# Layer 1's convolution in a four-layer graph network on one core: the product with adj² in two places a quarter, last sums by DMA and VectorE, 0/1 blocks as bytes

## The chip, the cores and the metric

The kernel runs as one program on one core of a Trainium2 chip. The metric is device time in microseconds (us); lower is better. The core has five engines that run their own instruction streams in order: TensorE (PE in the profile, with its weight loads as PEld), VectorE (DVE), ScalarE (ACT), GpSimd (POOL) and SyncE (SP), which issues most DMA transfers. An instruction that waits holds up everything behind it on its engine. SBUF is the on-chip memory of 128 partitions; matmul results land in PSUM, which has 8 banks of 128 partitions x 512 fp32 numbers.

## The reference

Four residual layers over x of shape (8, 2048, 64): 8 batches, 2048 nodes, 64 features. Each normalises x, applies a ReLU and adds a graph layer. adj is a 0/1 matrix of 2048 x 2048, sparse except near its first rows and columns. The change is in layer 1 and in how adj is kept for layers 1 and 2:

```python
def _L1_gnn_ref(x, A, embedding, weight, bias):
    K = weight.shape[1]                                  # 3
    w = jnp.einsum('nd,dkio->nkio', embedding, weight)   # d: 16
    b = jnp.einsum('nd,do->no', embedding, bias)
    As = [jnp.eye(N, dtype=x.dtype), A]
    As.append(2.0 * (A @ As[-1]) - As[-2])
    A_stack = jnp.stack(As, 0)
    x_g = jnp.einsum('knm,bmc->bnkc', A_stack, x)
    out = jnp.einsum('bnki,nkio->bno', x_g, w)
    return out + b

h = jnp.maximum(_layernorm(x, axis=-1), 0.0)
x = x + _L1_gnn_ref(h, adj, L1_gnn_embedding, L1_gnn_weight, L1_gnn_bias)
```

So each node has its own weights, a mix of 16 matrices by its embedding. Layer 2 multiplies adj with a message three times (`adj @ v`), with two small dense maps around it.

## The kernel before

**Layout.** Features lie on partitions in pairs of batches: 4 quarters q, each 128 partitions (2 batches x 64 features) by 2048 nodes. Nodes come in 16 target tiles of 128 and in 4 chunks of 512 (4 tiles). An array "by nodes" has 128 nodes on partitions and 512 columns (8 batches x 64).

**The sparse product** (class `Feed`). For one target tile t the product adj x is summed in one PSUM bank `acc`: first three dense source tiles (`dense`, the "hubs": 3 tiles, each in a high and a low part, so 6 matmuls), then `LISTED[t]` listed groups of 128 gathered source rows (7 to 3 for t from 1 to 15), each 2 matmuls; tile 0 takes 13 whole source tiles instead. A listed group is fetched into `raw` (POOL's indirect DMA, line 2578; for tile 0 SP's plain DMA, line 2576), split into `part_hi` (ACT, line 2595) and `part_lo` (DVE, line 2596), and multiplied with 0/1 weights. The weights are cast by ACT from adj blocks kept in bf16: `cells` and `zero` (line 2554) and `dense` (line 2564). `ahead` is how many groups are split before the one in use, `raws` how many fetch buffers there are, `group` how many blocks one cast takes. `finish` adds the node's own row (`own`, an SP load) and leaves `z`.

**The convolution** (`convolution_near`). `product(place)` computes adj (adj h) for one chunk, turned to features by four transposes a tile (`turn`) into `aah`. Chunk order is 1, 0, 2, 3 ("places" 0 to 3). While place p is convolved, `product(p + 1)` runs in between, cut into pieces by its `yield`s; `product(0)` runs alone, ahead of the loop.

In a place there are 4 quarters, and in each 4 block groups (`blk` 0, 2, 4, 6; two blocks of 2 embedding entries each). A block group is 4 PSUM banks `pk` (of 6): 4 matmuls with `w01` (128 rows) and, after a piece of the product, 4 with `w2` (64 rows each, on `aah`); an fp32 matmul shows as two passes. VectorE then does 4 times `y = (pk + bias) * emb` (line 1834), and GpSimd sums y into two accumulators `half` (line 1840; the first block needs no sum, the last block's two sums are VectorE's). There are 3 buffers for y. A block's 128 partitions are two embedding entries of 64 outputs, so a quarter ends with a sum over the two 64-partition halves of each accumulator: `fold_up` does it on TensorE with a 128 x 64 matrix `fold`, into the two halves of one PSUM bank, and VectorE adds that bank to x (line 1736).

**What sets the order.** `advance()` runs the pieces of the next product: 30 of a place's 32 hooks (two in each block group, one between the w01 and the w2 matmuls, one after) each take their even share of `pieces(place + 1)`, mostly one or none. `waiting` is a list of small functions run one at each block group's end (in the last place, two a group, with the 12 messages for layer 2 among them). It holds `fold_up` two group ends after its quarter's end, then `first` (store x, start the normalisation) and the rest of it. On top of this the framework's scheduler orders each engine's stream. The SP queue carries `own`, `raw` of tile 0, the embedding loads of the next place (line 1776, `q<-in_embT_dram` in the profile), and x in and out.

Of the kernel before, what the change touches and what calls it, by code (L numbers as in the profile page):

```python
# [7 lines left out]
F = mybir.dt.float32  # L8
BF = mybir.dt.bfloat16
# [10 lines left out]
P = 128  # L20
NB = 8
N = 2048
D = 64
NP = NB // 2
NT = N // P
R = P // NP
CW = 512
NC = N // CW
TC = CW // P
# [13 lines left out]
HUBS = 3  # L43
FAR = NT - HUBS
LISTED = [0, 7, 6, 5, 4, 4, 4, 4, 4, 4, 3, 3, 3, 3, 3, 3]
PLACE = [sum(LISTED[:t]) for t in range(NT + 1)]
F16 = mybir.dt.float16


COLS = ["a_node", "a_gn", "a_ge", "fcb", "av", "b1", "b2", "iv", "bias3"]  # L50
# [84 lines left out]
class Kernel:  # L135
# [1543 lines left out]
    def convolution_near(self, slots, k):  # L1679
        nc, tc, a = self.nc, self.tc, self.a  # L1680
        xe, xo = self.chebyshev(slots)
        lists, steps, ident = self.lists, self.steps, self.ident
        lo, hi = slice(0, D), slice(D, P)
# [3 lines left out]
        for i, order in enumerate(((0, 1), (1, 0))):  # L1687
            t = k.tile([P, DO], F, name=f"w01_{i}")
# [15 lines left out]
                a["bias1"].rearrange("(b j) o -> j o b", j=2)[j],  # L1704
            )

        fold = k.tile([P, D], F, name="fold")
        nc.vector.tensor_add(fold, ident[:, lo], ident[:, hi])

        with (  # L1710
            tc.tile_pool(reuse_waits="tile", name="conv", bufs=2) as w,
            tc.tile_pool(reuse_waits="tile", name="conv_ps", bufs=1, space=PSUM) as ps,
# [4 lines left out]
            chunks = [1, 0, 2, 3]  # L1717
            emb = slots.tile([P, NBLK, CW], F, name="emb", tag="q4")
            two = slots.tile([P, 2, NP, CW], F, name="two", tag="q5")
            aahs, x = (two[:, 0], w.tile([P, NP, CW], F, name="aah", bufs=1)), two[:, 1]  # L1720
            waiting = []
# [7 lines left out]
            def side():  # L1729
                return ps.tile([P, CW], F, name="side")  # L1730

            def fold_up(q, accs):
                po = side()
                for i, h in enumerate((lo, hi)):
                    self.mm(po[h], fold, accs[i])
                nc.vector.tensor_add(x[:, q], po, x[:, q])

            def message(t):
                pn = steps.first_message(v, t, bank())
                self.send(0, t, pn, lists.hub, w)  # L1740

            feed = Feed(
                self, lists, w, self.sent[1], None, raws=4, casts=2, ahead=1, group=2,
                targets=[ch * TC + i for ch in chunks for i in range(TC)],
            )

            def product(place):
                ch, aah = chunks[place], aahs[place % 2]

                def turn(i, z):  # L1750
                    pz = side().rearrange("p (q n) -> p q n", q=NP)
                    for q in range(NP):
                        nc.tensor.transpose(pz[:, q], z[:, q * P : (q + 1) * P], ident)
                    nc.scalar.copy(aah[:, :, i * P : (i + 1) * P], pz)

                last = None
                for i in range(TC):
                    t = ch * TC + i
                    own = feed.own(t)
                    acc = ps.tile([P, CW], F, name="acc")  # L1760
                    feed.dense(acc, t, lists.hub)
                    yield
                    for n, _ in enumerate(feed.listed(acc, t)):
                        if n == 1 and last is not None:
                            turn(*last)
                        yield
                    z = w.tile([P, CW], F, name="z")
                    feed.finish(z, own, acc, t)
                    last = i, z
                    yield  # L1770
                turn(*last)
# [10 lines left out]
                        ),  # L1782
                    )

            def pieces(place):
                targets = [chunks[place] * TC + i for i in range(TC)]
                return sum(2 + (LISTED[t] or FAR) for t in targets)

            for blk in range(0, NBLK, 2):
                load_emb(0, blk)  # L1790
            nc.sync.dma_start(x, self.xs[1][chunks[0]])
# [3 lines left out]
            for place, ch in enumerate(chunks):  # L1795
                s = slice(ch * CW, (ch + 1) * CW)
                aah = aahs[place % 2]
                ends = place == NC - 1
                ahead = iter(()) if ends else product(place + 1)
                many, hook = 0 if ends else pieces(place + 1), 0  # L1800

                def advance():
                    nonlocal hook
                    for _ in range(many * hook // 30, many * (hook + 1) // 30):
                        next(ahead, None)
                    hook += 1

                if ends:
                    for c in chunks[:-1]:
                        for t in range(c * TC, (c + 1) * TC):  # L1810
                            waiting.append(lambda t=t: message(t))
                for q in range(NP):
                    accs = [w.tile([P, CW], F, name="half", bufs=4) for _ in range(2)]
                    sides = list(enumerate(((xe, hi), (xo, lo))))
                    for blk in range(0, NBLK, 2):
                        pks = {}
                        for b in (blk, blk + 1):
                            for half, (src, h) in sides:
                                pk = bank()
                                pks[b, half] = pk  # L1820
                                c = slice(b * P, (b + 1) * P)
                                self.mm(pk, w01[half][:, c], src(q)[:, s], stop=False)
                        advance()
                        if ends and waiting:
                            waiting.pop(0)()
                        for b in (blk, blk + 1):
                            for half, (src, h) in sides:
                                c = slice(b * P, (b + 1) * P)
                                self.mm(pks[b, half], w2[h, c], aah[h, q], start=False)
                        for b in (blk, blk + 1):  # L1830
                            for half in range(2):
                                acc = accs[half]
                                y = acc if b == 0 else w.tile([P, CW], F, name="y", bufs=3)
                                nc.vector.scalar_tensor_tensor(  # L1834
                                    y, pks[b, half], bias[:, b : b + 1], emb[:, b],
                                    op0=OP.add, op1=OP.mult,
                                )
                                if b > 0:
                                    add = nc.vector if b == NBLK - 1 else nc.gpsimd
                                    add.tensor_add(acc, acc, y)  # L1840
                        if q == NP - 1 and not ends:
                            load_emb(place + 1, blk)
                        advance()
                        if waiting:
                            waiting.pop(0)()
                    waiting[:0] = [lambda: None, lambda q=q, accs=accs: fold_up(q, accs)]
                for _ in ahead:
                    pass
                std = w.tile([P, CW], F, name="std", tag="y", bufs=3)
                norm = self.norm_parts(ch, x, Part(v, s), Part(u, s), std, bank, write)  # L1850

                def first(place=place, ch=ch, norm=norm):
                    self.store_x(1, ch, x)
                    next(norm)
                    if place + 1 < NC:
                        nc.sync.dma_start(x, self.xs[1][chunks[place + 1]])

                waiting[2:2] = [first, lambda: None, lambda norm=norm: next(norm, None)]
# [513 lines left out]
class Lists:  # L2372
# [99 lines left out]
    def fill(self, pool, w):  # L2472

        nc = self.nc
        rows = self.kern.a["adjT"].rearrange("j (t n) -> (j t) n", n=P)
        self.cells = pool.tile([P, PLACE[NT], P], BF, name="cells")
        group, late = 4, []

        def keep(s, n, raw):
            self.kern.behind(nc.vector.tensor_tensor(  # L2480
                self.cells[:, s], raw, self.there[:, s].unsqueeze(2).to_broadcast([P, n, P]),
                op=OP.mult,
            ))

        for c in range(0, PLACE[NT], group):
            n = min(group, PLACE[NT] - c)
            raw = w.tile([P, group, P], F, name="listed_raw", bufs=4)[:, :n]
            for i in range(n):
                self.kern.behind(nc.gpsimd.indirect_dma_start(  # L2489
                    raw[:, i], None, rows,  # L2490
                    bass.IndirectOffsetOnAxis(ap=self.cell[:, c + i : c + i + 1], axis=0),
                ))
            late.append((slice(c, c + n), n, raw))
            if len(late) > 2:
                keep(*late.pop(0))
            yield
        for x in late:
            keep(*x)
        yield

    def open(self, pool):
        self.dense = pool.tile([P, HUBS, N], BF, name="dense")
        self.zero = pool.tile([P, FAR, P], BF, name="zero")
        self.hub = Hub(pool, "hub")

    def load(self, w):
# [623 lines left out]
```

## Time and profile before

| | |
|---|---|
| median of 6 runs | 1979.81 us |
| lowest, highest | 1972.23, 1984.59 us |
| the profiled execution | 1974.29 us |
| its span, first to last instruction | 1972.5 us |
| mean granted TensorE clock | 0.911 |
| layer 1's convolution with `product(0)`, about | 735 to 1268 us of the span |
| `raw<-sent,index` gathers | 300, 1050 ns of POOL each |
| loads `dense_raw` of 1024 KB | 3, 5.9 us to landing each |

"Span" is the time between the first and the last instruction of the profiled execution. A row of a group of instructions reads: line of the kernel, engine, operation, output<-inputs, partitions x elements and types, count, then busy time and mean ns of one, then how long the engine stood idle just before these instructions and what ended the idle time. In a stage table each pair is busy us and, in brackets, the number of instructions. In a timeline a row is start, duration, engine, line and what it does; several alike in a row are merged.

### The profile page before, as it was taken

The page shows a single profiled execution, that of the slowest core. Times are in us where ns is not written, and L with a number is a line of the kernel's source. Part 1 is how long each engine was busy: PE and PEld are TensorE (multiplying, and loading weights), DVE is VectorE, ACT ScalarE, POOL GpSimd, SP SyncE. Part 2 cuts the span into 40 slices and gives each one's busy share as a digit, 9 for nine tenths or more (in the row PEclk, how much of TensorE's full clock was granted, in tenths as well). Part 3 has the DMA queues.
Part 4 walks back from the last instruction along what each step waited for, and adds up shares of the span by engine and source line. Part 5 has one row for each costly group of instructions (what it writes and reads, how often), then busy time and mean ns, then how long its engine had stood idle before and what let it go on. Part 6 is the DMA issues. An engine that isn't in the chain of part 4 may idle for free. (4 is left out here: it accounts for less than half of the span.)

```text
span 1972.5 us, 22337 instructions
## 1 busy us (share of the span) xinstructions
PE 1698.7 (86%) x7066; PEld 970.0 (49%) x7066; DVE 1409.5 (71%) x2389; ACT 809.6 (41%) x1627; POOL 1030.3 (52%) x959
## 2 busy tenths in 40 slices
PE   6859889998997787999999999769889998679875
PEld 2425666665324554444443444447667565345432
DVE  6778778884677674877677557589889676458864
ACT  5712344454664653221121010256566754267300
POOL 1100166776870753875765545266474641478760
PEclk8868899998996898999999989789989999689887
DMA  9740223345335876233141210378788774666655
GB/s 345 263 120 1 77 75 103 111 125 180 99 101 173 246 228 177 81 91 107 49 117 33 70 48 38 110 217 253 244 260 268 231 257 168 225 177 176 182 173 190
DMA packets 124057, 305.20 MB, mean 155 GB/s; under 512 B 29312, under 2 KB 31120, under 8 KB 118160
## 3 DMA queue, kind: packets, MB, share of 16 engines
q0 software_dynamic: 45328, 149.60, 25.3%
q1 hardware_dynamic: 76288, 149.80, 22.7%
q10 hardware_dynamic: 2304, 4.20, 0.6%
q8 instruction: 59, 0.97, 0.2%
q14 instruction: 78, 0.64, 0.1%
HBM read 240.40 MB, written 63.14 MB: 154 GB/s over the span
## 5 line engine op out<-in xcount | busy, mean ns | idle before, releaser
L2578 POOL DMA_INDIRECT raw<-sent,index x300 | 315.1, 1050 | 304.8 <-DVE part_lo L2596 117.8
L2596 DVE TENSOR_TENSOR part_lo<-raw,part_hi 128x512 fp32r<-128x512 f32 x352 | 265.4, 776 | 120.9 <-ACT part_hi L2595 113.8
L2595 ACT CAST part_hi<-raw 128x512 fp32r<-128x512 f32 x352 | 212.6, 619 | 312.2 <-PE acc L176 211.2
L1840 POOL TENSOR_TENSOR half<-half,y 128x512 f32<-128x512 f32 x192 | 247.2, 1316 | 134.1 <-DVE y L1834 129.0
L176 PE MATMUL pk<-q,w 128*128 128x512 f32 (+1 forms) x768 | 301.8, 610 | 2.3 <-DVE q L1724 0.9
L176 PE MATMUL acc<-q,ident 128*128 128x512 f32 x416 | 203.0, 614 | 24.3 <-DVE q L2909 16.2
L176 PE MATMUL acc<-part_hi,weights 128*128 128x512 f32 x365 | 175.5, 484 | 28.0 <-ACT part_hi L2595 26.7
L1834 DVE SCALAR_TENSOR_TENSOR y<-pk,bias,q 128x512 f32<-128x512 f32 x224 | 158.0, 743 | 52.1 <-PE pk L176 33.0
L176 PEld LDWEIGHTS pk<-q,w 128*128 128x128 f32 (+1 forms) x768 | 115.9, 190 | 156.1 <-issue 120.8
L176 PE MATMUL acc<-part_lo,weights 128*128 128x512 f32 x365 | 165.9, 456 | 24.1 <-DVE part_lo L2596 23.6
L2819 POOL DMA_INDIRECT ring<-f_rows,near x121 | 140.1, 1158 | 66.5 <-issue 28.3
L176 PEld LDWEIGHTS acc<-q,ident 128*128 128x128 f32 x416 | 77.5, 195 | 98.5 <-issue 44.5
L2305 POOL TENSOR_TENSOR q<-q,beta 128x512 f32<-128x512 f32 x57 | 76.0, 1336 | 72.4 <-DVE beta L2281 33.8
L176 PEld LDWEIGHTS acc<-part_hi,weights 128*128 128x128 f32 x365 | 73.0, 200 | 78.1 <-ACT part_hi L2595 43.8
L176 PEld LDWEIGHTS acc<-part_lo,weights 128*128 128x128 f32 x365 | 72.9, 200 | 75.2 <-DVE part_lo L2596 60.3
L176 PE MATMUL pp<-adj,x_ind_hi 128*128 128x512 f32 x256 | 89.3, 464 | 0.5 <-DVE q L846 0.3
L2564 ACT CAST hub_weights<-dense 128x384 fp32r<-128x384 bf16 x80 | 40.6, 511 | 103.7 <-PE acc L176 99.2
L2890 DVE TENSOR_TENSOR q<-ring,e 128x1024 f32<-128x1024 f32 x58 | 70.0, 1217 | 9.3 <-PE acc L176 9.1
L2305 POOL TENSOR_TENSOR q<-q,coef 128x512 f32<-128x512 f32 x57 | 63.0, 1106 | 21.0 <-DVE q L2328 17.6
L176 PE MATMUL pp<-adj,x_ind_lo 128*128 128x512 f32 x256 | 72.7, 403 | 0.0
L287 DVE RECIPROCAL std<-std 128x512 f32<-128x512 f32 x16 | 53.6, 3350 | 25.3 <-ACT std L286 21.3
L2489 POOL DMA_INDIRECT listed_raw<-in_adjT_dram,cell x60 | 62.9, 1048 | 16.5 <-issue 15.6
(503 smaller groups left out, 3421.5 us busy)
## 6 DMA issues: line engine op xcount, KB each, us to landing
rows<-in_adj_dram SPq DMA_DIRECT2D x16, 1024.0 KB, 9.4
adj_t<-in_adjT_dram SPq DMA_DIRECT2D x64, 256.0 KB, 3.0
own<-sent SPq DMA_DIRECT2D x52, 256.0 KB, 4.2
raw<-sent SPq DMA_DIRECT2D x52, 256.0 KB, 3.7
sent<-u SPq DMA_DIRECT2D x48, 256.0 KB, 3.6
q<-x SPq DMA_DIRECT2D x10, 1024.0 KB, 5.2
x<-q SPq DMA_DIRECT2D x9, 1024.0 KB, 3.9
links<-squares POOLq DMA_DIRECT2D x16, 512.0 KB, 8.8
```

Of the source, the lines that this page charges most:

```text
L176: self.nc.tensor.matmul(out, lhsT, rhs, start=start, stop=stop)
L287: nc.vector.reciprocal(std, std)
L1834: nc.vector.scalar_tensor_tensor(y, pks[b, half], bias[:, b : b + 1], emb[:, b], op0=OP.add, op1=OP.mult,)
L1840: add.tensor_add(acc, acc, y)
L2305: self.nc.gpsimd.tensor_tensor(x, x, by.unsqueeze(2).to_broadcast([P, NB, D]), op=OP.mult)
L2489: self.kern.behind(nc.gpsimd.indirect_dma_start(raw[:, i], None, rows, bass.IndirectOffsetOnAxis(ap=self.cell[:, c + i : c + i + 1], axis= ...
L2564: self.nc.scalar.copy(to, self.lists.dense[:, :, i * P : (i + 1) * P])
L2578: self.nc.gpsimd.indirect_dma_start(raw, None, self.rows[:], bass.IndirectOffsetOnAxis(ap=self.lists.index[:, c : c + 1], axis=0),)
L2595: nc.scalar.copy(hi, raw)
L2596: nc.vector.tensor_sub(lo, raw, hi.bitcast(F))
L2819: self.nc.gpsimd.indirect_dma_start(to, None, self.kern.f_rows[:], bass.IndirectOffsetOnAxis(ap=index, axis=0))
L2890: nc.vector.tensor_tensor(y.rearrange("n i (b f) -> n i b f", b=NB), block[:, i : i + 2, : NB * D].rearrange("n i (b f) -> n i b f", b=NB) ...
```

## The change

1. **The product in two places of a quarter.** A target tile's product now yields once in the middle of its listed groups and once at its end (tile 0: three times and at its end), and the loop takes one such part between the w01 and the w2 matmuls of the block groups 0 and 4 (in the first quarter before chunk 0: of all four). The second place in a block group is gone. `Feed` splits 3 groups ahead instead of 1 and casts 4 blocks at a time instead of 2; so there are 4 part buffers of each kind instead of 2 and 2 buffers of `own` instead of 1.
2. **The last sums.** The matrix `fold` and its matmuls are gone. At a quarter's end two SP transfers move the upper half of the first accumulator and the lower half of the second into a tile `other`, each to the opposite partitions (64 partitions x 512 numbers each, 128 KB). VectorE adds the two halves that lie right to x (64 x 512 each), and then `other` (128 x 512).
3. **Bytes.** `cells`, `dense` and `zero` are kept in uint8 instead of bf16.

```diff
+U8 = mybir.dt.uint8
-        fold = k.tile([P, D], F, name="fold")
-        nc.vector.tensor_add(fold, ident[:, lo], ident[:, hi])
-            def fold_up(q, accs):
-                po = side()
+            def cross(accs):
+                other = w.tile([P, CW], F, name="other", bufs=1)
+                nc.sync.dma_start(other[lo], accs[0][hi])
+                nc.sync.dma_start(other[hi], accs[1][lo])
+                return other
+
+            def fold_up(q, accs, other):
                 for i, h in enumerate((lo, hi)):
-                    self.mm(po[h], fold, accs[i])
-                nc.vector.tensor_add(x[:, q], po, x[:, q])
+                    nc.vector.tensor_add(x[h, q], accs[i][h], x[h, q])
+                nc.vector.tensor_add(x[:, q], other, x[:, q])
...
-                self, lists, w, self.sent[1], None, raws=4, casts=2, ahead=1, group=2,
+                self, lists, w, self.sent[1], None, raws=4, casts=2, ahead=3,
...
                     feed.dense(acc, t, lists.hub)
-                    yield
+                    stops = [LISTED[t] // 2 - 1] if t else [2, 6, 9]
                     for n, _ in enumerate(feed.listed(acc, t)):
-                        if n == 1 and last is not None:
+                        if n in stops:
+                            yield
+                        if n == stops[0] and last is not None:
                             turn(*last)
-                        yield
                     z = w.tile([P, CW], F, name="z")
                     feed.finish(z, own, acc, t)
                     last = i, z
                     yield
...
-                many, hook = 0 if ends else pieces(place + 1), 0
-
-                def advance():
-                    nonlocal hook
-                    for _ in range(many * hook // 30, many * (hook + 1) // 30):
-                        next(ahead, None)
-                    hook += 1
...
-                        advance()
+                        if blk % 4 == 0 or (q == 0 and chunks[(place + 1) % NC] == 0):
+                            next(ahead, None)
...
-                        advance()
                         if waiting:
                             waiting.pop(0)()
-                    waiting[:0] = [lambda: None, lambda q=q, accs=accs: fold_up(q, accs)]
+                    waiting[:0] = [
+                        lambda: None,
+                        lambda q=q, accs=accs, other=cross(accs): fold_up(q, accs, other),
+                    ]
...
-        self.cells = pool.tile([P, PLACE[NT], P], BF, name="cells")
+        self.cells = pool.tile([P, PLACE[NT], P], U8, name="cells")
...
-        self.dense = pool.tile([P, HUBS, N], BF, name="dense")
-        self.zero = pool.tile([P, FAR, P], BF, name="zero")
+        self.dense = pool.tile([P, HUBS, N], U8, name="dense")
+        self.zero = pool.tile([P, FAR, P], U8, name="zero")
```

In the stream that VectorE gets, the scheduler puts the third add (of `other`) directly behind the second half add at 11 of the 16 quarter ends; at the other 5 between 1 and 6 instructions stand between them. In SP's stream the two transfers stand together at 11 quarter ends; at the last quarter of places 0 to 2 they stand among the next place's embedding loads, and at the first two of place 3 a message's store stands between them. Outside the convolution the order of the five streams is unchanged.

More of the change, by code (lines that the diff above doesn't have):

```diff
@@ L1783, in load_emb @@
                     )
-            def pieces(place):
-                targets = [chunks[place] * TC + i for i in range(TC)]
-                return sum(2 + (LISTED[t] or FAR) for t in targets)
             for blk in range(0, NBLK, 2):
```

## Prediction

> **What bounds the kernel now.** I read the stage table of the span first, then the costliest groups of the convolution, then the timelines of TensorE and VectorE there.
>
> ```profile
> 785.00:905.00 120.00, 117.74 (x381) 53.24 (x379) 94.25 (x112) 28.91 (x59) 91.64 (x75) 1.00 0.30 88
> 905.00:1012.00 107.00, 106.08 (x338) 44.21 (x338) 76.82 (x96) 17.69 (x35) 71.87 (x60) 1.00 0.26 79
> 1012.00:1125.00 113.00, 111.96 (x357) 46.50 (x354) 76.36 (x100) 14.80 (x29) 67.19 (x55) 1.00 0.20 59
> 1125.00:1250.00 125.00, 121.44 (x394) 51.59 (x393) 77.84 (x127) 10.32 (x18) 62.59 (x52) 0.95 0.13 47
> ```
>
> The columns are the stretch, its length, busy us of PE, PEld, DVE, ACT, POOL, then the granted clock and DMA. The four stretches are places 0 to 3. TensorE is busy for 97 to 99% of each, at a full clock in the first three: it sets the time. VectorE is next, at 79% in place 0 and 62 to 72% after it.
>
> ```profile
> 1001.47 3.70 PE L176 MATMUL pk<-q,w 128*128 128x512 f32 x8
> 1005.10 1.99 PE L176 MATMUL pk<-aah,w 64*128 64x512 f32 x8
> ...
> 1014.46 3.59 PE L176 MATMUL pk<-q,w 128*128 128x512 f32 x8
> 1017.49 0.80 PE L176 MATMUL acc<-part_hi,weights 128*128 128x512 f32 x1
> 1018.13 0.40 PE L176 MATMUL acc<-part_lo,weights 128*128 128x512 f32 x1
> 1018.46 1.99 PE L176 MATMUL pk<-q,w 64*128 64x512 f32 x8
> 1020.37 1.08 PE L176 MATMUL side<-half,fold 128*64 128x512 f32 x4
> 1021.38 3.70 PE L176 MATMUL pk<-q,w 128*128 128x512 f32 x8
> ```
>
> Here the starts matter, since matmuls overlap. The fold of a quarter takes 21.38 - 20.37 = 1.01 us. A block group without a piece takes 3.63 (1001.47 to 1005.10) + 1.92 us.
>
> ```profile
> 838.54 0.50 PE L176 MATMUL acc<-part_lo,weights 128*128 128x512 f32 x1 [2.18 <-DVE part_lo L2596]
> 1008.53 1.74 DVE L1840 TENSOR_TENSOR half<-half,y 128x512 f32<-128x512 f32 x1
> 1010.19 0.74 DVE L1834 SCALAR_TENSOR_TENSOR y<-pk,bias,q 128x512 f32<-128x512 f32 x1
> 1011.03 0.69 DVE L1840 TENSOR_TENSOR half<-half,y 128x512 f32<-128x512 f32 x1
> 1012.20 1.41 DVE L1834 SCALAR_TENSOR_TENSOR half<-pk,bias,q 128x512 f32<-128x512 f32 x2 [0.47 <-PE pk L176]
> ```
>
> First, the one long stall of TensorE on the product. Then a seam between two quarters on VectorE: the quarter's last w2 matmuls end at 1007.0, its last sum at 1011.72, 4.7 us later, and VectorE has 0.5 us left before the next quarter's first bank.
>
> ```profile
> L2596 DVE TENSOR_TENSOR part_lo<-raw,part_hi 128x512 fp32r<-128x512 f32 x55 | 68.4, 1255 | 31.2 <-ACT part_hi L2595 31.2
> L1840 DVE TENSOR_TENSOR half<-half,y 128x512 f32<-128x512 f32 x32 | 36.2, 1135 | 8.4 <-POOL half L1840 6.5
> L1736 DVE TENSOR_TENSOR q<-side,q 128x512 f32<-128x512 f32 x15 | 10.2, 679 | 0.0
> ...
> sent<-u SPq DMA_DIRECT2D x12, 256.0 KB, 2.0
> own<-sent SPq DMA_DIRECT2D x8, 256.0 KB, 2.6
> ```
>
> These are groups and transfers between 785 and 1250 us. A VectorE add of two SBUF tiles takes 1.1 to 1.3 us on average here, 0.69 alone; the fold's add, which reads PSUM, takes 0.68. The last column of the transfers is us from issue to landing.
>
> **Part 1, the fold off TensorE.** 16 folds of 1.01 us go. The last lies in the tail after 1244 us, where TensorE waits; 15 count: -15.2 us.
>
> **Part 2, the pieces.** Do fewer, larger pieces cost TensorE less? Between w01 and w2 a piece of two matmuls takes 0.97 us (1017.49 to 1018.46), but the w01 run ahead of it shrinks from about 3.5 (after another piece) to 3.03: net some 0.47. In a stream a matmul takes 0.23 (the six of a dense part from 1012.96 to 14.46 with the change-over). So a piece costs what its matmuls cost, wherever it stands: 0 for the lumps.
>
> **Part 3, three groups ahead.** The stall at 838.54 goes (-2.2). In `product(0)`, from 743 to 780 us, TensorE idles 7.5 us on part_hi, and in 0.5 us bits 4.6 on part_lo weight loads; four gather buffers still set the pace (POOL waits 15.9 us there for part_lo, to fetch again), so I take -3 of a bound of 0 to -6.
>
> **Part 4, what the new sums cost VectorE.** 48 adds for 16: at 0.69 each +22 us, at the 1.48 that three part_lo from 791.44 took each during GpSimd's sums (4.43 us) +60, over places with 25 to 47 us idle each. Not bound on average, but at the seams. Take one between quarters of places 1 and 2. A half add (64x512 adds at 611 us took 0.71) now precedes the last sum, so that ends 5.4 us after w2. The second transfer follows. No SBUF-to-SBUF transfer is in the trace: 2.0 us (`sent<-u`, out of SBUF, twice the bytes) to 4.5 (the embedding loads on the same queue). I take 2.0 as the nearest row. Then the add of `other` ends at 5.4 + 2.0 + 0.7 = 8.1, and one split behind it at 8.8. TensorE meanwhile runs 3.03 + a lump of ten matmuls 2.34 + 1.92 = 7.3, then two matmuls of 0.86 into the two spare banks, and then needs VectorE's first read (0.74) to be over: it must start by about 8.3. Stall 0.5 at 6 seams: 3.0. In place 0 the last sums already come 6.0 to 7.6 us after w2, 2 later, with two splits behind `other` and a lump of twelve: 2.5 at 3 seams, 7.5. In place 3 there is no split and no lump but a message (0.99): needed by 7.3, there at 8.1, 0.8 at 2 seams, 1.6. That is the wait that queues: behind `other` stand the next quarter's y, behind them GpSimd's sums, and TensorE's banks. The 5 other ends have work in between: 0, but 1.0 at the change to place 3, where two embedding loads of 1.97 us of SP stand ahead of the transfer and `first` needs x. Together +13.1.
>
> In the tail the last sum now ends at 1247.6, + 2.0 to 4.5 + 0.7 = 1250.3 to 1252.8 against 1251.7 before: 0.
>
> The Trainium skill says that GpSimd's SBUF interfaces are shared with VectorE, with contention when a DVE instruction has two SBUF inputs (GPSIMD Engine Reference, "1. Specifications"). The rows above agree (1255 and 1135 against 679 ns), and it speaks against this edit, which trades a PSUM input for SBUF ones. If every new add paid the contended 1.48, each seam would end about 1.6 us later, +18 us at 11 seams; I don't take it, since GpSimd has finished its sums at most seams.
>
> **Part 5, bytes.** ACT's 128x512 casts take 0.62 us from fp32 (line 2595) and 0.61 from bf16 (line 2554): width is no cost, so 0 for 209 casts; an ACT at 41% covers small changes. The three 128x2048 `dense` casts on VectorE (1.23 us) lie on a chain, as one buffer is reloaded after each, and TensorE waits 4.3 us for the last at 632.9. At one number per step (four 128x512 adds of 0.69) each would take 2.8: 0 to +4.6. They run at twice that rate today, and their input is unchanged: 0. A gain has no source, as the reads stay.
>
> The Trainium skill ties VectorE's double rate for a single source to both tiles lying in SBUF, with even sizes, not to the type (VectorE: DVE Perf Modes, "What auto-detection actually checks"). No run here shows a byte output yet; by it the sum keeps 0.
>
> **Sum.** -15.2 - 2.2 - 3 + 13.1 = -7.3 us. The profiled execution took 1974.29, so 1967.0; it stands 5.5 below the median of the runs, 1979.81, which would become 1972.5. I predict that median.
>
> **The rivals.**
> *The seams are hidden.* If the last sums come 1 us earlier (in the old trace one comes at 4.4 after w2), the 13.1 falls to near 2 and `product(0)` gains 6: -15.2 - 2.2 - 6 + 2 = -21, 1958.5. For it: two spare banks. Against: VectorE's 79% in place 0. Chance 0.15.
> *VectorE becomes the bound at the seams.* One mechanism: the add of `other` waits at the head of VectorE's stream for a transfer. If landing takes 4.5 instead of 2.0, 11 seams cost 2.5 more each, +27.5: +20, 2000. It ends slower than before once landing passes about 2.7 us (7.3 / 11 = 0.66 more). For it: 2.6 for `own` in the same stretch, and the scheduler's order. Against: 128 KB is small, and the queue holds few other loads. At 3.2 us it gives +6. Chance 0.27.
> *The edit gives back what it takes.* Landing 2.6 and a little contention: 1979. For it: two numbers of near 15 with opposite signs. Chance 0.18.
> *It doesn't do what it says* (byte casts slower, parts starved): the casts at twice their time would put some 100 us on ACT; nothing in the rows speaks for it, 0.02, in the slower case.
>
> **How the numbers follow.** The forecast, -3 to -15 us, has 0.38. A measurement of this kernel can tell about 0.3% (5.9 us) from no change. Faster: 0.15 and 0.31 of the forecast's 0.38 = 0.46. Within: the rest of the forecast, 0.07, most of the third rival, 0.14, and 0.07 of the second's low end = 0.28. Slower: 0.26. The range reaches from 1958, the first rival, to 1993, a landing near 3.9 us (1972.5 + 11 x 1.9). The forecast's own is 1965 to 1977.
>
> **What would show it.** Right: no `side<-half,fold`, places 1 and 2 shorter by 1 to 4 us each, VectorE idle before `q<-other,q` about 1 to 2 us at 11 seams, released by DMA; no stall near 838. Wrong: that idle at 3 us or more and TensorE waiting for y at each seam; lumps that make TensorE wait on part_lo; `dense` casts above 1.3 us; byte casts on ACT slower than 0.63.

## The result, and the profile after

The changed kernel took 1993.58 us (median of 20 runs, 1981.47 to 2000.0), the kernel before 1979.8 on the same chip (41 runs). The ratio is 1.0061, with a 95% interval of 1.0046 to 1.0077: slower by about 12 us, where I had forecast faster by 7. The profiled execution after has a span of 1985.5 us.

The place of the loss shows at a glance. From the first dense matmul of `product(0)` to layer 2's first weight matmul ("the convolution" from here on) the two traces have 535.3 and 547.5 us; all the rest of the span differs by 0.8 us. First the stage table of the changed kernel, over the same pieces of work as the table of before (columns: stretch, its length, busy us of PE, PEld, DVE, ACT, POOL, granted clock, DMA).

```profile
787.00:914.00 127.00, 114.84 (x361) 51.24 (x361) 95.43 (x115) 26.00 (x51) 89.77 (x78) 0.99 0.32 89
914.00:1028.00 114.00, 107.78 (x322) 44.73 (x319) 82.83 (x99) 15.80 (x30) 70.41 (x59) 0.96 0.26 79
1028.00:1138.00 110.00, 108.22 (x340) 45.90 (x340) 79.19 (x108) 12.49 (x23) 64.30 (x53) 1.00 0.20 62
1138.00:1264.00 126.00, 115.93 (x378) 49.99 (x377) 85.35 (x138) 11.60 (x20) 63.69 (x54) 0.97 0.18 57
```

The four places were 120, 107, 113 and 125 us long. Places 0 and 1 each became 7 us longer, place 2 became 3 shorter, place 3 about 1 longer. TensorE was busy 98% of place 0 before and is busy 90% now: its folds are gone, and 12 us without work stand where there were 2. VectorE is no fuller in place 0 (95.43 against 94.25 us). And the clock, 1.00 in places 0 to 2 before, is 0.96 in place 1. Next, VectorE's groups and the new transfer, between 785 and 1264 us.

```profile
L2591 DVE TENSOR_TENSOR part_lo<-raw,part_hi 128x512 fp32r<-128x512 f32 x51 | 65.2, 1299 | 13.3 <-ACT part_hi L2590 8.8 <-PE acc L177 4.3
L1833 DVE TENSOR_TENSOR half<-half,y 128x512 f32<-128x512 f32 x32 | 36.4, 1139 | 4.4 <-POOL half L1833 3.4
L1738 DVE TENSOR_TENSOR q<-half,q 64x512 f32<-64x512 f32 x32 | 21.8, 681 | 0.5
L1739 DVE TENSOR_TENSOR q<-other,q 128x512 f32<-128x512 f32 x15 | 11.0, 730 | 25.0 <-DMA other<-half 23.5 <-issue 1.5
...
other<-half SPq DMA_DIRECT2D x32, 128.0 KB, 2.2
```

The new adds cost what I had taken, 0.68 and 0.73 us, and the landing is 2.2 us against my 2.0. VectorE stands idle 23.5 us in front of the add of `other`, in 14 waits. So the prices were right, and the wait is where it was expected. What it does to TensorE shows at one seam of place 1; three timelines, of VectorE, TensorE and GpSimd.

```profile
990.99 0.75 DVE L1827 SCALAR_TENSOR_TENSOR y<-pk,bias,q 128x512 f32<-128x512 f32 x1 [2.06 <-POOL half L1833]
991.65 3.51 DVE L2591 TENSOR_TENSOR part_lo<-raw,part_hi 128x512 fp32r<-128x512 f32 x1
995.09 2.05 DVE L1827 SCALAR_TENSOR_TENSOR y<-pk,bias,q 128x512 f32<-128x512 f32 x3
997.74 1.76 DVE L1833 TENSOR_TENSOR half<-half,y 128x512 f32<-128x512 f32 x1 [0.60 <-POOL half L1833]
...
1000.68 0.68 DVE L1833 TENSOR_TENSOR half<-half,y 128x512 f32<-128x512 f32 x1
1001.39 0.69 DVE L1738 TENSOR_TENSOR q<-half,q 64x512 f32<-64x512 f32 x1
1003.71 0.69 DVE L1739 TENSOR_TENSOR q<-other,q 128x512 f32<-128x512 f32 x1 [1.63 <-DMA other<-half]
1004.32 0.69 DVE L2591 TENSOR_TENSOR part_lo<-raw,part_hi 128x512 fp32r<-128x512 f32 x1
1004.92 1.40 DVE L1827 SCALAR_TENSOR_TENSOR half<-pk,bias,q 128x512 f32<-128x512 f32 x2
```

```profile
991.04 1.99 PE L177 MATMUL pk<-aah,w 64*128 64x512 f32 x8
...
1001.58 1.98 PE L177 MATMUL pk<-q,w 128*128 128x512 f32 x4
1005.72 3.05 PE L177 MATMUL pk<-q,w 128*128 128x512 f32 x4 [2.16 <-DVE half L1827]
```

```profile
989.68 4.93 POOL L1833 TENSOR_TENSOR half<-half,y 128x512 f32<-128x512 f32 x4
995.44 0.97 POOL L2573 DMA_INDIRECT raw<-sent,index  x1 [0.82 <-DVE part_lo L2591]
996.42 2.51 POOL L1833 TENSOR_TENSOR half<-half,y 128x512 f32<-128x512 f32 x2
```

The quarter's last w2 matmuls end at 993.0. My seam had the last sum end 5.4 us later; it ends 8.3 us later (1001.36), and `other` is added by 1004.40, 11.4 after w2 instead of 8.1. The 3.5 us for one split (0.69 elsewhere) is most of the difference: it starts at 991.65, while GpSimd works through four sums (989.68 to 994.61), and ends 0.55 us after the last of them. Then comes the wait of 1.63 for the landing, behind it the next quarter's first banks, and TensorE waits 2.16 us for those. What follows that stall is in the table by single microseconds, whose column before the last two is the granted clock.

```profile
1004.00:1005.00 1.00, 0.00 (x0) 0.00 (x0) 1.00 (x3) 0.00 (x0) 0.00 (x0) 1.00 0.00 0
1005.00:1006.00 1.00, 0.28 (x1) 0.28 (x2) 1.00 (x3) 0.00 (x0) 0.72 (x1) 1.00 0.00 0
1006.00:1007.00 1.00, 1.00 (x3) 0.36 (x3) 1.00 (x3) 0.00 (x0) 0.24 (x1) 0.75 0.12 20
1007.00:1008.00 1.00, 1.00 (x3) 0.19 (x1) 0.64 (x1) 0.00 (x0) 0.94 (x1) 0.50 0.72 201
1008.00:1009.00 1.00, 1.00 (x3) 0.30 (x4) 0.00 (x0) 0.00 (x0) 1.00 (x2) 0.50 0.17 57
1009.00:1010.00 1.00, 1.00 (x4) 0.49 (x4) 0.00 (x0) 0.00 (x0) 0.55 (x1) 0.55 0.45 162
```

After the stall TensorE's clock is halved for 3.4 us, which costs 1.7 more. I had this nowhere in my sum.

### The profile page after: what moved, and what is told of

Read it like the earlier page. It is cut to its first block, busy times and chain, and to the rows that moved or that the text cites. A ratio compares the mean times of both kernels' runs of the same rounds, so it can differ in the third digit from the quotient of the medians.

```text
span 1985.5 us, 22302 instructions
## 1 busy us (share of the span) xinstructions
PE 1689.4 (85%) x7002; PEld 973.5 (49%) x7002; DVE 1431.1 (72%) x2420; ACT 806.0 (41%) x1608; POOL 1029.1 (52%) x959
## 5 line engine op out<-in xcount | busy, mean ns | idle before, releaser
L177 PE MATMUL pk<-q,w 128*128 128x512 f32 (+1 forms) x768 | 310.9, 622 | 24.0 <-DVE half L1827 11.3
L1833 POOL TENSOR_TENSOR half<-half,y 128x512 f32<-128x512 f32 x192 | 241.3, 1286 | 122.7 <-DVE y L1827 118.1
L177 PE MATMUL acc<-q,ident 128*128 128x512 f32 x416 | 202.7, 614 | 23.6 <-DVE q L2904 17.4
L177 PE MATMUL acc<-part_hi,weights 128*128 128x512 f32 x365 | 166.2, 458 | 27.4 <-ACT part_hi L2590 26.7
L2559 ACT CAST hub_weights<-dense 128x384 fp32r<-128x384 uint8 x80 | 40.6, 511 | 115.4 <-PE acc L177 110.8
```

The source lines that it names most:

```text
L177: self.nc.tensor.matmul(out, lhsT, rhs, start=start, stop=stop)
L2559: self.nc.scalar.copy(to, self.lists.dense[:, :, i * P : (i + 1) * P])
```

## The experiments

The runs were on chips where the kernel before took 2037.7, 2037.6, 1981.5 and 2026.0 us; each ratio is against its runs on the same chip. The chips differ outside the convolution: e1's stretch behind it is 750 us against 702 before, while its places 1 to 3 are equal to before's within 0.1 us each. On the slower chips a kernel's runs also scatter by some 30 us. So the convolution in the trace is the finer scale; it is one execution for each kernel. It scatters too, by up to some 4 us: the two executions of the changed kernel (the first and e5) differ by 2.4 us, and e8 and e11 by 4.0 over places 0 and 1, where their work and its order are the same. A difference of that size is not shown by one pair of traces.

In the table "idle" is time without a running matmul, from the first `pk` matmul on: in places 0 to 3, and in the tail behind the last. "Half" counts stretches of 3.4 us at half clock from place 0's first w2 matmuls to layer 2 (the sum of one minus the granted clock over single microseconds, divided by 1.7; it comes out whole).

| kernel | convolution us | idle, places | idle, tail | half | ratio to before, 95% |
|---|---|---|---|---|---|
| before | 535.3 | 10.2 | 8.8 | 7 | |
| changed | 547.5 | 29.6 | 12.0 | 11 | 1.0061 (1.0046 to 1.0077) |
| e5 changed, again | 545.1 | 32.2 | 12.0 | 8 | 1.0051 (1.0016 to 1.0085) |
| e1 bytes | 536.5 | 10.4 | 8.8 | 7 | 1.0000 (0.9974 to 1.0026) |
| e7 bytes, three ahead | 533.1 | 8.7 | 9.7 | 6 | 1.0015 (0.9979 to 1.0052) |
| e2 and lumps | 536.7 | 14.9 | 8.7 | 5 | 1.0006 (0.9981 to 1.0031) |
| e10 e2, one-source splits | 529.4 | 8.7 | 8.8 | 7 | 0.9959 (0.9941 to 0.9976) |
| e3 e7 and the new sums | 544.2 | 28.3 | 13.2 | 9 | 1.0009 (0.9980 to 1.0038) |
| e6 e3, three adds held | 537.7 | 24.5 | 12.9 | 7 | 1.0052 (1.0018 to 1.0086) |
| e9 e3, third add held | 533.0 | 22.1 | 12.6 | 10 | 0.9979 (0.9959 to 0.9998) |
| e4 changed, three adds held | 535.1 | 21.2 | 12.1 | 10 | 0.9976 (0.9946 to 1.0006) |
| e8 changed, third add held | 530.0 | 16.8 | 12.3 | 8 | 0.9964 (0.9940 to 0.9988) |
| e11 e8, last quarter folded | 525.3 | 17.7 | 8.9 | 6 | 0.9964 (0.9936 to 0.9992) |
| e12 e8, four last sums | 526.5 | 17.7 | 12.7 | 7 | 0.9991 (0.9964 to 1.0018) |

**Which part loses (e1 to e4).** Three theories. A: VectorE's wait for the landing, at the head of its stream, makes the loss. B: the lumps make it, with splits that stand alone and late. C: neither alone, only both together. To "hold" an add means to keep it behind what stands before it in the program, where the scheduler would draw it forward.

e1 is the kernel before with `U8` for `cells`, `dense` and `zero`.

> Part 5 alone: the 0/1 blocks as bytes, all else as before. The casts of the trace after the change took what they took before (128x512 on ACT 0.62 us), and no stage outside the convolution became longer. All theories expect no difference: -2 to +2 us against the kernel before. A loss of 5 us or more would mean that the bytes bear part of the +12 us, through something that the rows of the casts do not show.

Measured: 1.0000, and each of places 1 to 3 within 0.1 us of before. The bytes bear nothing.

e2 is the changed kernel with `fold`, its matmuls and its add put back, and without `cross`:

```diff
...
-            def fold_up(q, accs, other):
+            def fold_up(q, accs):
+                po = side()
                 for i, h in enumerate((lo, hi)):
-                    nc.vector.tensor_add(x[h, q], accs[i][h], x[h, q])
-                nc.vector.tensor_add(x[:, q], other, x[:, q])
+                    self.mm(po[h], fold, accs[i])
+                nc.vector.tensor_add(x[:, q], po, x[:, q])
...
```

> Parts 2, 3 and 5 without part 4: the product in two places of a quarter and three groups ahead, the fold on TensorE as before. Theory A (VectorE's wait for the transfer at the quarter ends makes the loss): without that wait the lumps cost nothing, 0 to -4 us against the kernel before. Theory B (the lumps make the loss: few splits left, each alone and late in VectorE's stream behind GpSimd's queue of sums, and z late): slower than before by 8 to 20 us, since the fold's 15 us of TensorE stay too. Theory C (only both together cost, as a late split moves the last sum and so the transfer): -3 to +5.

Measured: +1.4 us in the convolution. Theory B falls: the lumps don't make the loss. Whether they are free is not shown. Against e7, which differs in the lumps alone, e2 has +3.6 us, with 6.2 us more idle time in the places. Three other comparisons differ in the lumps alone: +3.3 (changed less e3; +0.9 with e5), -2.6 (e4 less e6) and -3.0 (e8 less e9).

e3 is e7 (below) with `cross` and the new `fold_up`.

> Parts 3, 4 and 5 without part 2: the new last sums by transfer and VectorE and three groups ahead, but the product in 30 even shares as before. Theory A: the wait at the head of VectorE's stream is still there at each quarter end, so slower than before by 5 to 15 us. Theory B: the splits are spread again, the fold's 15 us are gone and only the seams that I forecast remain: 5 to 12 us faster than before. Theory C: 5 to 15 us faster.

Measured: +8.9 us in the convolution. Theories B and C fall; in the trace the new sums lose without any lumps. The ratio of the whole (0.9980 to 1.0038) neither shows nor excludes this loss.

e4 keeps the program's order on VectorE for the three adds:

```diff
-                    nc.vector.tensor_add(x[h, q], accs[i][h], x[h, q])
-                nc.vector.tensor_add(x[:, q], other, x[:, q])
+                    self.behind(nc.vector.tensor_add(x[h, q], accs[i][h], x[h, q]))
+                self.behind(nc.vector.tensor_add(x[:, q], other, x[:, q]))
```

> The changed kernel whole, but its three last adds keep the program's order in VectorE's stream: they stand behind the y of block group 2 of the next quarter, 10 us after the transfer was issued, so VectorE waits for no landing at the quarter's end. Theory A: the idle 24 us ahead of the third add go, and 8 to 15 us of time with them: 0 to 5 us faster than before. Theory B: the late splits stay, so it gains 3 us or less against the changed kernel and stays 8 us or more slower than before. Theory C: most of the loss goes, 0 to 10 us faster than before.

Measured: -0.2 us against before and -12.4 against the changed kernel, by the order of 48 instructions. As theory A has it, though at the low end. The whole runs agree: 0.9976 against the changed kernel's 1.0061, with intervals that don't meet. What it still lacks shows in its groups.

```profile
L1738 DVE TENSOR_TENSOR q<-half,q 64x512 f32<-64x512 f32 x32 | 43.1, 1346 | 0.5
...
L1739 DVE TENSOR_TENSOR q<-other,q 128x512 f32<-128x512 f32 x15 | 19.0, 1269 | 0.5
```

No idle time is left in front of the third add. But the same half adds that took 681 ns at the quarter's end take 1346 here, beside GpSimd's sums.

**Does it repeat, and where should the adds stand (e5 to e9)?**

> The changed kernel again, beside the kernel before and the two that follow, on one chip: the convolution, from its first dense matmul to layer 2's first weight matmul, took 547.5 us against 535.3 in the first two traces. If that difference is the order of the work and not of one execution, it comes again: 12 us more than before in that stretch, to within 3, with extra stretches of half clock on TensorE after its stalls.

Measured: +9.8 us in the convolution, ratio 1.0051. The idle time is the same within 3 us; the trace has 8 stretches of half clock where the first had 11. So the loss is the kernel's, and some of it varies with the clock.

e6 is e3 with the edit of e4.

> Parts 3, 4 and 5 without part 2, and the three last adds kept behind the next quarter's y. It differs from e3_pieces_sums in VectorE's order alone. Theory A (the wait at the head of VectorE's stream): the four stalls of 2.3 to 2.8 us at the ends of quarters in place 0 go, and the half clock after them: 8 to 14 us less than e3 in the convolution (530 to 536 us against 544.2). Theory D (VectorE is simply too full there, with 22 us more of adds): the adds cost the same wherever they stand, and it stays within 3 us of e3.

Measured: 537.7, 6.5 less than e3, outside both ranges. The whole runs don't show this gain: on the same chip e6's median is 2043.6 us and the changed kernel's 2044.2 (e5), and the traced execution of e6 was the fastest of its 12. In the trace the wait is gone, and a new one came. VectorE and GpSimd in e6, in place 0:

```profile
891.11 3.78 DVE L1738 TENSOR_TENSOR q<-half,q 64x512 f32<-64x512 f32 x1
...
895.59 0.68 DVE L1739 TENSOR_TENSOR q<-other,q 128x512 f32<-128x512 f32 x1
```

```profile
890.62 3.71 POOL L1843 TENSOR_TENSOR half<-half,y 128x512 f32<-128x512 f32 x3
```

A half add of 0.68 us that starts 0.5 us after GpSimd began three sums ends 0.56 us after them, and the y behind it are late.

e7 is the kernel before with bytes, `ahead=3` and four blocks a cast.

> Parts 3 and 5 alone: three groups split ahead, four blocks a cast, the product in 30 shares and the fold on TensorE as before. My prediction gave part 3 -2.2 us for the one long stall of place 0 and -3 in the first product. The rows of the trace after the change showed the first and not the second, so: -1 to -4 us in the convolution against before. If three ahead itself starves the product's other steps, it is 0 to +5.

Measured: -2.2 us, less than the scatter. The stall at 838 is gone (places 0 to 3 idle 8.7 against 10.2 us). From the first dense matmul of `product(0)` to place 0's first matmul it takes 17.4 us, 16.4 before: nothing gained there.

e8 puts the half adds where GpSimd is done, and the third add where its tile has landed:

```diff
-            def cross(accs):
+            def cross(q, accs):
...
+                for i, h in enumerate((lo, hi)):
+                    nc.vector.tensor_add(x[h, q], accs[i][h], x[h, q])
                 return other
-            def fold_up(q, accs, other):
-                for i, h in enumerate((lo, hi)):
-                    nc.vector.tensor_add(x[h, q], accs[i][h], x[h, q])
-                nc.vector.tensor_add(x[:, q], other, x[:, q])
+            def fold_up(q, other):
+                self.behind(nc.vector.tensor_add(x[:, q], other, x[:, q]))
...
```

> The changed kernel with one difference: the two half adds stay at the quarter's end, and the add of the tile that the transfers bring is kept behind the y of the next quarter's block group 2. In e4, where all three were kept back, 15 of 32 half adds took over 1.5 us (1.35 on average), since GpSimd was summing then; at the quarter's end each took 0.68. Theory A with that price: the half adds cost 0.68 again and no landing is waited for, so 2 to 6 us less than e4 in the convolution (529 to 533 against 535.1), 12 to 18 less than the changed kernel. If a half add's place doesn't matter: 534 to 537.

Measured: 530.0 us, and 0.9964 (0.9940 to 0.9988): faster than before by about 7 us, and so faster than both kernels. The order of the convolution's instructions, on all engines, differs from the changed kernel's in the third add alone (and in one small step of VectorE in place 3). The seam shown above, in e8's VectorE:

```profile
994.02 0.69 DVE L1735 TENSOR_TENSOR q<-half,q 64x512 f32<-64x512 f32 x1
994.74 0.69 DVE L2591 TENSOR_TENSOR part_lo<-raw,part_hi 128x512 fp32r<-128x512 f32 x1
995.35 1.40 DVE L1827 SCALAR_TENSOR_TENSOR half<-pk,bias,q 128x512 f32<-128x512 f32 x2
...
1002.09 1.08 DVE L1739 TENSOR_TENSOR q<-other,q 128x512 f32<-128x512 f32 x1
```

The split follows the half add at once, the next quarter's first banks are read 0.6 us after its start, and `other` comes 7 us after that. TensorE runs its next eight `pk` matmuls through, without the stall.

e9 is the same for e3.

> The same place for the adds, with the product in 30 shares (no lumps). In e6, with all three kept back, half adds took up to 3.8 us. Theory A with the price of the place: 5 to 12 us less than e6 (526 to 533 against 537.7), that is 0 to 7 less than e7, which keeps the fold on TensorE (533.1). Theory D (VectorE is too full with the added sums wherever they stand): 536 to 539.

Measured: 533.0, at the edge of theory A's range and against theory D. It does no better than e7, which keeps the fold: with 30 pieces the third add met GpSimd's sums more often (7 of 16 took over 1.5 us, 2 in e8) and idle time in the places is 22.1 us.

**What the remaining waits are (e10 to e12).** e10 is e2 with the convolution's splits (those with `ahead=3`) as plain copies, so its result is not the layer's:

```diff
-            nc.vector.tensor_sub(lo, raw, hi.bitcast(F))
+            if self.AHEAD == 3:
+                nc.vector.tensor_copy(lo, raw)
+            else:
+                nc.vector.tensor_sub(lo, raw, hi.bitcast(F))
```

> As e2_lumps, but the low part of each gathered row in the convolution is a plain copy of the row instead of row minus high part: one SBUF input instead of two (that part of the result is left out). The theory that a VectorE instruction with two SBUF inputs waits until GpSimd has no sum left, and that this makes the lumps cost: no split takes over 1 us, TensorE's gaps in places 0 and 1 (10.3 and 3.6 us in e2) shrink to 4 to 7 and about 1, and the convolution takes 528 to 533 us against 536.7. The rival, that lumps starve because their splits stand late in VectorE's order, whatever they cost: 535 to 538.

Measured: 529.4, and idle time in places 0 and 1 of 6.5 and 1.6 us, as the theory had it. But its criterion fell: three of the 53 copies took over 1 us, two of them 3.05 and 3.25, and ended 0.28 to 0.29 us after a run of GpSimd's sums. One SBUF input doesn't protect a copy. Most copies (0.41 us) were quick; the scheduler set about half of them elsewhere, in threes and fours, and they are shorter, by some 14 us in all. So this doesn't tell their price from their place.

e11 keeps TensorE's fold for the last quarter alone.

> As e8, but the very last quarter of the convolution is folded by TensorE as before the change. At that end nothing else hides the way of the sums: TensorE waited 7.0 us there for the add of the transferred tile in every trace with the new sums and 3.5 us in every one with the fold. If the transfer is the cause of the difference: 2 to 3.5 us less than e8 in the stretch from the last place's first centring matmul to layer 2 (29.4 us in e8, 28.5 before), nothing elsewhere. If the tail is set by the normalisation behind it: no difference.

Measured: the idle time shrank as expected (tail 12.3 to 8.9), but the stretch only from 29.4 to 28.8, of which one stretch of half clock less is 1.7. The fold's matmuls and the centring behind them stand in that time instead. My expectation missed.

```profile
1239.67 1.12 PE L177 MATMUL pk<-q,center 128*128 128x512 f32 x2
1244.54 1.07 PE L177 MATMUL side<-half,fold 128*64 128x512 f32 x2 [3.74 <-DVE half L1842]
1245.54 2.00 PE L177 MATMUL pk<-q,center 128*128 128x512 f32 x2
1247.47 1.84 PE L177 MATMUL side<-half,fold 128*64 128x512 f32 x2
```

The other 4 us by which e11 is below e8 lie in places 0 and 1, which have the same order of work in both: idle time is nearly equal there (15.3 and 14.4 us), but e8 has a stretch of half clock in place 1 and more of it at the start of place 0. That is the size of chance in this scale.

e12 is e8 with one line changed:

```diff
-                                    add = nc.vector if b == NBLK - 1 else nc.gpsimd
+                                    add = nc.vector if b >= NBLK - 2 else nc.gpsimd
```

> As e8, but VectorE makes the last four sums of a quarter instead of the last two (32 sums of 0.69 us more on VectorE, 22 us, and 32 of 1.24 less on GpSimd). In all traces so far each VectorE instruction that has its tiles in SBUF and meets a run of GpSimd's sums ends 0.55 us after one of GpSimd's ends; 13 or 14 of the 32 last sums take 1.76 us for it, and the splits ahead of the last block group 3.5. If that waiting, not VectorE's own work, sets the seams of place 0: last sums of 0.69, TensorE's gaps in places 0 and 1 (10.8 and 3.6 us in e8) smaller by 3 to 8 us in all, 524 to 529 us against 530.0. If VectorE's load sets them: the 22 us more make it 531 to 540.

Measured: 526.5, which is in the first theory's range, but not for its reason. The last sums do run at 0.69 (row below), yet idle time in places 0 and 1 is 15.1 us against 14.4, not 3 to 8 less, and e11 reached 525.3 without this edit. The 3.5 us splits ahead of the last block group are still there, 7 of them over 3 us. Neither theory is shown.

```profile
L1833 DVE TENSOR_TENSOR half<-half,y 128x512 f32<-128x512 f32 x64 | 43.0, 693 | 1.4
```

## Why the prediction was wrong

The mechanism that decides is the second rival's: the add of `other` waits at the head of VectorE's stream, and the next quarter's y queue behind it. e8 shows it, since moving that add alone turns +12 us into -7. Its condition was wrong, though: I had it pass zero at a landing of 2.7 us, and it lost 12 at 2.2.

| term | forecast us | shown |
|---|---|---|
| fold off TensorE | -15.2 | -4.3 for the four of place 2 (e8: 114.8 to 110.5 us, from the last w2 matmul of place 1 to that of place 2) |
| waits at the seams | +13.1 | 14.7 and 17.3 us of idle time in the places (changed and e5, less e2) |
| lumps | 0 | +3.6 (e2 less e7), -2.6 (e4 less e6), -3.0 (e8 less e9) |
| three ahead: stall, `product(0)` | -2.2, -3 | -2.2 in all (e7); `product(0)` 0 |
| tail | 0 | against before +3.2 us idle |
| bytes | 0 | 0 (e1; `dense` casts 1226 ns against 1227, ACT 0.62 us) |
| half clock | not in the sum | against before +6.8 (4 stretches), +1.7 in e5 |

**Part 4 is the step that failed: "Together +13.1" for the new sums, with 0 for the tail.** e2 is the changed kernel with the fold put back, so the two differ in parts 1 and 4 alone. My sum for these was -15.2 + 13.1 = -2.1 us. The convolution shows +10.8 (changed less e2) and +8.4 (e5 less e2), and without lumps +11.1 (e3 less e7). The whole runs show the first (1.0061 against 1.0006, with intervals that don't meet), not the last (1.0009 against 1.0015). With the fold at its forecast, the new sums cost 23.6 to 26.3 us and not 13.1. TensorE's idle time in the places is only a little above the forecast; what I had at nothing came on top: 3.3 us of idle time in the tail, and 6 and 3 more stretches of half clock (changed and e5, less e2), 10.2 and 5.1 us. These terms add up to some 2 us more than measured: some of the half clock falls on waiting, and the 16th fold left the tail. Most of the cost hangs on the third add: with it alone held, the +10.8 becomes -6.7 (e8 less e2). The other parts (2, 3 and 5), forecast at -5.2, show +1.4 (e2).

**The fold** went as forecast, and so did the price of an add and of the landing.

**The seams** came near their sum in part by luck. At eight of them `other` is added 8.0 to 8.1 us after w2, as forecast, and TensorE loses 0 to 0.7 us there, none of it at three seams of place 2 where I had 0.5 each. It loses more at the three of place 0, 2.9 to 3.5 us each and not 2.5, and at the seam of place 1 shown above, 3.1 and not 0.5. In that one a lone split in front of the last block group is stretched, and the last sum ends 8.3 us after w2 and not 5.4. I had read 4.7 from one seam of the old trace and moved it by the half add's 0.7 alone.

**"So a piece costs what its matmuls cost, wherever it stands: 0 for the lumps"** is neither shown nor refuted: the pairs above have both signs and lie within the scatter. But the lumps were priced on TensorE alone, and VectorE's splits move with them: with lumps 9 take over 3 us in the changed kernel and 7 each in e2 and e8, without them 3 before, 4 in e7 and 2 in e9 (but 7 in e3). Their sum did not grow (68.3 us in the changed kernel, 71.1 before); single ones stand where GpSimd has a queue of sums.

**The -3 in `product(0)`** failed: that stretch took 16.4 us before and 16.7 after. I had noted that four gather buffers set its pace and then not followed it; they are still four.

**The tail's 0** failed too: TensorE waits 6.96 us ahead of the last centring matmuls, where it waited 3.46 before. I compared the end of the last add, which is unchanged, and not what TensorE could do meanwhile: the fold let it go on with half of its work. TensorE in the tail, before and after:

```profile
1246.29 1.35 PE L176 MATMUL side<-half,fold 128*64 128x512 f32 x2 [3.46 <-DVE half L1840]
1247.58 2.08 PE L176 MATMUL pk<-q,center 128*128 128x512 f32 x2
```

```profile
1265.15 2.07 PE L177 MATMUL pk<-q,center 128*128 128x512 f32 x2 [6.96 <-DVE q L1739]
```

**The clock.** A stall was priced at its own length. I read places 0 to 2 at a clock of 1.00 and took it as given. The rule that bears on this stands in the Trainium skill ("TensorE: Matmul & The Clock Gate", "Part 1: The HAM clock gate (the "warmup" mystery)"): the array falls to half rate after an idle window of about 3.4 us, and the window runs freely. The halves and the 3.4 us agree with the rows here, the length of the stalls does not: in places 0 to 2 the longest stall in the 8 us before a stretch of half clock was 0.9 to 3.4 us, and others of 1.7 to 2.8 us were followed by none. The stall of 2.16 us shown above stands in e5 too (2.14 us), without a half clock behind it; and two of the four stretches in places 0 and 1 of the changed kernel follow a stall of 0.88 us.

What stays open: whether the lumps cost anything by themselves, and how much of that is the splits' place and how much z (VectorE waits 15.0 us for `acc` there in the changed kernel, 5.7 before); and what decides whether a stall halves the clock.

## What to carry to other kernels

Price a moved or added instruction at the place where the scheduler puts it, not by its duration elsewhere: here the same adds gave +12 or -7 us. An instruction that waits for a transfer belongs behind the work that TensorE's banks depend on, and an SBUF-to-SBUF add where GpSimd has no sums queued. When the tight engine is freed of work, count what the freed time turns into, a stall's clock included.

## What the runs showed of the hardware

In the changed kernel each VectorE instruction with all its tiles in SBUF that meets a run of GpSimd's sums stretches, and ends 0.55 to 0.56 us after the end of one of GpSimd's sums or of the whole run: 0.69 us become 1.76, 3.5 or 4.0. Of the 54 splits of the changed kernel 15 met such sums and took 2.77 us on average; the 39 others took 0.69 at most. Copies of 0.41 us stretched too (3.05 and 3.25 in e10). An instruction that reads PSUM did not: 132 y ran beside GpSimd's sums, none over 0.75 us, and in the kernel before 11 of the 16 fold adds did, none over 0.69. The adds that stand in the fold's place were stretched where they met the sums: half adds to 1346 ns on average in e4, the third add to 1438 in e8, against 679 for the fold's add.
